# Outputs and gates by feature instead of by token, with the norm's factors sent through DRAM

## The chip, the cores and the metric

The kernel runs on one core of a Trainium2 chip. The metric is device time in microseconds (us) of one execution; lower is better. Beside the runs there is one profiled execution, whose trace gives each instruction's start and length on the engines: PE (TensorE; PEld is its weight load), DVE (VectorE), ACT (ScalarE), POOL (GpSimd), and SP (SyncE), which here issues nearly all DMAs.

## The reference, cut to what matters

x has 16 samples of 128 tokens and 256 features. A small attention layer makes h from x. Then comes the part that the change is in, a gated delta rule with 16 key heads and 32 value heads of 128 features each; two value heads share a key head. Its result is normalised over the 128 features of a head, weighted, gated by silu(z), and projected back to 256 features:

```python
mixed = hidden_states @ W_qkv
z = (hidden_states @ W_z).reshape(b, s, NV, DV)
beta = jax.nn.sigmoid(hidden_states @ W_b)
g = -jnp.exp(A_log) * jax.nn.softplus(hidden_states @ W_a + dt_bias)
mixed = jax.nn.silu(_causal_conv(mixed, conv_w))
...
core = _chunk_gated_delta_rule(q, k, v, g, beta)
core = core * jax.lax.rsqrt(jnp.mean(core * core, axis=-1, keepdims=True) + EPS) * norm_w
core = core * jax.nn.silu(z)
return core.reshape(b, s, VAL_DIM) @ W_out
```

Inside the rule, q and k are divided by their lengths, and each sample's 128 tokens need the inverse of a triangular 128x128 matrix for each head. Two feed-forward layers follow. All is float32.

## The kernel before

The work of the delta rule is cut into 64 units. A unit is one key head (`kh`) and one group of four samples (`g`), which makes eight pairs (`NP`, sample and value head) of 128 tokens. Every unit goes through the same stages, and the main loop (L872) is a software pipeline: in slot n, unit n does its first stage (`keys`, L451), unit n-1 its decays, unit n-7 (`MERGE`) the merging of the inverse and its values, unit n-8 (`OUT`) its outputs (L750), and unit n-10 (`LAST`) its projection (`finish_unit`, L801). Within a slot `plan` gives each step a time on a scale of 24, and the steps are written out in the order of these times. A scheduler then moves single instructions, so that the built program's order on an engine is near the plan but not the same. Each engine runs its own instructions in the built order and waits where an operand or a buffer isn't ready. Buffers turn over in pools: `ps_b` has six buffers of PSUM that almost every product takes one of.

The inverse of the triangular matrices is done for four units at once, on 32x32 blocks, by DVE with some help of POOL (`inverse`, L566). It is spread over two slots in every four: `first` in slot n where n-5 is a multiple of four, `second` in the slot after.

The steps that the change touches, in a unit's order:

- `square` and `norms` (L465, L469): ACT squares keys and queries, PE adds over the features by a product with a matrix of ones 32 columns wide, one for each block of 32 tokens. The sums come out on 32 partitions for each block, all alike; DVE's 32x32 transpose (`turned`, L475) turns them so that a partition holds the sums of its own token. `factors` (L477) makes nn of the query's sum on POOL, 128x4.
- `logarithms` (L498): one block on ACT with the table of exponent and logarithm, for three units at once: the decays of unit n-1, r of unit n-9 (r to the power -1/2 by Ln and Exp), lk and kn of unit n. All silu of the slot stand before or after the block, since they need another table.
- `gate` (L755): z = silu(h W_z), tokens on partitions, two samples to a call; four matmuls with 256 moving columns each. A float32 matmul of the program stands in the profile as two instructions.
- `new_values` (L766), `attend` (L776): PE forms y and then the output of the rule, tokens on partitions, four pairs to a call. ACT squares each pair from PSUM and adds up along the features (`accum_out`, one more instruction each) into r, 128x8. DVE multiplies by z.
- `root` (L790): POOL adds nn to r. `norm` (L795): POOL multiplies z by r, which is one number for each token and pair.
- `turn` (L806): PE transposes z's eight 128x128 tiles, ACT copies them to SBUF as zT, scaled by the norm's weight `nw`, which is one number for each feature. `project` (L813): PE multiplies zT by W_out and adds up over the key heads in PSUM.

On SP the loads of weights (w_qk, w_v, w_gate, wo_head), of decays (aT, 512 KB to all partitions) and the moves of blocks of 32 columns (diag, W, T) stand in one queue, in the built order; an issue that waits holds back those behind it.

Of the kernel before, what the change touches and what calls it, by code (L numbers as in the profile page):

```python
# [56 lines left out]
def tile_adaln_attn_ffn(  # L57
# [80 lines left out]
    sums = dram.tile([NG, NK * NP, S], F32, name="sums")  # L138

# [7 lines left out]
    def attention():  # L147
# [144 lines left out]
        def output(g):  # L292
# [14 lines left out]
            def logs():  # L307
# [12 lines left out]
                V.tensor_tensor(a, ps[:, :, NV:], dtb[:, None, :].to_broadcast([P, GS, NV]), ALU.add)  # L320
                A.activation(sp, sp, AF.Ln, bias=one)
# [129 lines left out]
    def keys(u):  # L451
# [17 lines left out]
        def norms():  # L469

            ps = ps_b.tile([P, 2 * GS, BL], F32, name="ps_n", tag="b")
            for b in BLOCKS:
                T.matmul(ps[b], lhsT=ones, rhs=d["sqa"][:, :, :, b], start=True, stop=True)
            d["tr"] = pc.tile([P, 2 * GS, BL], F32, name="turned", tag="turned")
            V.transpose(out=d["tr"].rearrange("p s t -> p (s t)"), in_=ps.rearrange("p s t -> p (s t)"))  # L475

        def factors():  # L477
            tr = d["tr"][:, :, 0].rearrange("p (s j) -> p j s", j=2)

            nn = d["nn"] = pc.tile([P, GS], F32, name="nn", tag="nn", bufs=10)  # L480
            G.tensor_scalar(nn, tr[:, 1, :], 1e-6, P * P * 1e-6, ALU.add, ALU.mult)  # L481
# [14 lines left out]
        return [lambda: qk(0), lambda: qk(1), lambda: silu(0), lambda: silu(1), square, norms, factors, fade]  # L496

    def logarithms(new, old, done):  # L498
# [17 lines left out]
        if new:  # L516
            block.append(A.activation(lk, un[new]["tr"][:, :, 0].rearrange("p (s j) -> p j s", j=2)[:, 0, :], AF.Ln, bias=small))
            block.append(A.activation(kn, lk, AF.Exp, scale=0.5))
# [231 lines left out]
    def outputs(u):  # L750
# [4 lines left out]
        def gate(n):  # L755
            if n == 0:
                d["z"] = late["p"].tile([P, NP, S], F32, name="z", tag="z", bufs=3)
            ps = ps_b.tile([P, 2, 2 * S], F32, name="ps_z", tag="b")
            for j in range(2):
                t0 = (2 * n + j) * S  # L760
                for c in range(ND):
                    T.matmul(ps[:, j, :], lhsT=hTs[g][:, c, t0 : t0 + S], rhs=w_gate[u][:, c, :],  # L762
                             start=c == 0, stop=c == ND - 1)
            silu_of(d["z"][:, 4 * n : 4 * n + 4, :].rearrange("p q f -> p (q f)"), ps.rearrange("p s f -> p (s f)"))
# [11 lines left out]
        def attend(n):  # L776
            ps = ps_b.tile([P, 4, S], F32, name="ps_ot", tag="b")
            for j in range(4):
                p = 4 * n + j
                T.matmul(ps[:, j, :], lhsT=d["aT"][:, p, :], rhs=d["y"][:, p, :], start=True, stop=True)  # L780
            if n == 0:
                d["r"] = late["p"].tile([P, NP], F32, name="r", tag="r", bufs=2)
            for j in range(4):
                p = 4 * n + j
# [3 lines left out]
            V.tensor_tensor(z, ps, z, ALU.mult)  # L788

        def root():  # L790

            r = d["r"].rearrange("p (s h) -> p s h", h=2)
            G.tensor_tensor(r, r, d["nn"][:, :, None].to_broadcast([P, GS, 2]), ALU.add)

        def norm():  # L795
            G.tensor_tensor(d["z"], d["z"], d["r"][:, :, None].to_broadcast([P, NP, S]), ALU.mult)  # L796

        return [lambda: gate(0), lambda: gate(1), lambda: new_values(0), lambda: new_values(1),
                lambda: attend(0), lambda: attend(1), root], norm

    def finish_unit(u):  # L801
# [4 lines left out]
        def turn(n):  # L806
            ps = ps_b.tile([P, 4, S], F32, name="ps_zt", tag="b")
            for j in range(4):
                T.transpose(ps[:, j, :], d["z"][:, 4 * n + j, :], ident)
            d["zT", n] = late["p"].tile([P, 4, S], F32, name="zT", tag="zT", bufs=2)  # L810
            A.activation(d["zT", n], ps, AF.Copy, scale=nw)  # L811

        def project(n):  # L813
# [3 lines left out]
            for j in range(2):  # L817
                for h in range(2):
                    T.matmul(ps[:, j, :], lhsT=d["zT", n][:, 2 * j + h, :], rhs=w_o[u][:, h, :],  # L819
                             start=kh == j == h == 0, stop=kh == NK - 1 and j == h == 1)  # L820
# [10 lines left out]
        return [lambda: turn(0), lambda: turn(1), lambda: project(0), lambda: project(1)]  # L831
# [40 lines left out]
    for n in range(N + LAST):  # L872
# [298 lines left out]
```

## Time and profile before

| What | us |
| --- | --- |
| runs, median (lowest to highest of 3) | 2407.47 (2407.19 to 2407.93) |
| the profiled execution's own time | 2408.48 |
| its span, first to last instruction | 2406.8 |
| PE busy in the span | 2194.9 (91%) |
| PEld busy | 1432.5 (60%) |
| DVE busy | 1605.2 (67%) |
| ACT busy | 1482.6 (62%) |
| POOL busy | 755.0 (31%) |
| DMA, share of 16 engines (hardware queue) | 22.2% |

Three parts follow one another: the attention stage and the first units' first stages (to about 310 us), the steady pipeline of slots (to about 1980 us), and the feed-forward layers (from about 2020 us). A busy share is a mean over all three. In the lists of instructions a line reads: line of the kernel, engine, operation, output tile <- input tiles, shapes, count | busy us in all, mean ns of one | idle time of the engine just before, and what ended it. In a timeline a line begins with its start and its length, both in us, and ends in brackets with the idle time before it and what released it. Matmuls overlap one another by some 0.15 us, so what a step takes on PE is read from its start to the next step's start.

### The profile page before, as it was taken

The page shows a single profiled execution, that of the slowest core. Times are in us where ns is not written, and L with a number is a line of the kernel's source. Part 1 is how long each engine was busy: PE and PEld are TensorE (multiplying, and loading weights), DVE is VectorE, ACT ScalarE, POOL GpSimd, SP SyncE. Part 2 cuts the span into 40 slices and gives each one's busy share as a digit, 9 for nine tenths or more (in the row PEclk, how much of TensorE's full clock was granted, in tenths as well). Part 3 has the DMA queues.
Part 4 walks back from the last instruction along what each step waited for, and adds up shares of the span by engine and source line. Part 5 has one row for each costly group of instructions (what it writes and reads, how often), then busy time and mean ns, then how long its engine had stood idle before and what let it go on. Part 6 is the DMA issues. An engine that isn't in the chain of part 4 may idle for free. (4 is left out here: it accounts for less than half of the span.)

```text
span 2406.8 us, 41884 instructions
## 1 busy us (share of the span) xinstructions
PE 2194.9 (91%) x16248; PEld 1432.5 (60%) x16248; DVE 1605.2 (67%) x2094; ACT 1482.6 (62%) x3382; POOL 755.0 (31%) x575
## 2 busy tenths in 40 slices
PE   6898588989999998989999998989899898999999
PEld 3443255766666666767666666767666776344445
DVE  4677879687887869697887869696877831311111
ACT  4666576867777686868677776768677774111110
POOL 4555423243323324143323323242323213600000
PEclk9899889999999999999999999999999999999999
DMA  2200031323323332323232232323222324000000
GB/s 57 91 14 23 22 89 51 76 66 81 72 65 80 84 83 61 77 66 83 75 87 71 62 78 61 87 64 80 74 79 68 82 57 145 5 1 20 9 1 18
DMA packets 289908, 148.35 MB, mean 62 GB/s; under 512 B 184240, under 2 KB 278192, under 8 KB 289712
## 3 DMA queue, kind: packets, MB, share of 16 engines
q1 hardware_dynamic: 287792, 141.44, 22.2%
q0 software_dynamic: 1344, 4.20, 0.5%
q8 instruction: 130, 2.13, 0.4%
q14 instruction: 66, 0.54, 0.1%
q10 hardware_dynamic: 576, 0.05, 0.0%
HBM read 119.13 MB, written 5.51 MB: 52 GB/s over the span
## 5 line engine op out<-in xcount | busy, mean ns | idle before, releaser
L446 DVE SCALAR_TENSOR_TENSOR cv<-ps_in,cw,cv 128x500 f32<-128x500 f32 (+2 forms) x768 | 548.1, 737 | 62.8 <-ACT cv L444 51.3
L435 PE MATMUL ps_in<-hT,w_qk 128*128 128x512 f32 x512 | 274.1, 660 | 20.8 <-PE ps_lo L688 7.0
L444 ACT ACTIVATE cv<-ps_in,cw 128x512 f32<-128x512 f32 x256 | 174.7, 682 | 159.1 <-PE ps_in L435 154.1
L762 PE MATMUL ps_z<-w_gate,hT 128*128 128x256 f32 x1024 | 258.5, 387 | 12.3 <-DVE cv L446 12.3
L435 PE MATMUL ps_in<-hT,w_v 128*128 128x512 f32 x512 | 247.7, 607 | 5.0 <-DVE z L788 3.0
L819 PE MATMUL ps_out<-wo_head,zT 128*128 128x256 f32 x1024 | 245.7, 380 | 1.2 <-ACT zT L811 1.2
L819 PEld LDWEIGHTS ps_out<-wo_head,zT 128*128 128x128 f32 x1024 | 192.8, 191 | 53.5 <-issue 28.3
L788 DVE TENSOR_TENSOR z<-ps_ot,z 128x512 f32<-128x512 f32 x128 | 87.5, 684 | 201.9 <-ACT sq L786 201.9
L762 PEld LDWEIGHTS ps_z<-w_gate,hT 128*128 128x128 f32 x1024 | 180.3, 190 | 35.8 <-DVE cv L446 14.5
L796 POOL TENSOR_TENSOR z<-z,r 128x1024 f32<-128x1024 f32 x64 | 148.9, 2327 | 139.6 <-ACT r L515 123.7
L481 POOL TENSOR_SCALAR nn<-turned 128x4 f32<-128x4 f32 x64 | 12.5, 196 | 561.3 <-DVE turned L475 560.8
L786 ACT ACTIVATE sq<-ps_ot 128x128 f32<-128x128 f32 x512 | 142.1, 278 | 58.1 <-PE ps_ot L780 52.1
L597 POOL TENSOR_TENSOR prod<-inv,gm 128x2048 f32<-128x2048 f32 x16 | 89.0, 5564 | 230.7 <-DVE gm L644 230.7
L435 PEld LDWEIGHTS ps_in<-hT,w_v 128*128 128x128 f32 x512 | 96.8, 198 | 106.6 <-issue 96.9
L435 PEld LDWEIGHTS ps_in<-hT,w_qk 128*128 128x128 f32 x512 | 94.7, 206 | 97.6 <-issue 77.8
L549 PE MATMUL ps_kq<-kq 128*128 128x256 f32 x512 | 138.0, 393 | 10.2 <-DVE cv L446 9.7
L780 PE MATMUL ps_ot<-y,aT 128*128 128x128 f32 x1024 | 138.9, 280 | 1.2 <-ACT y L774 1.2
L553 DVE TENSOR_TENSOR bT<-ps_kq,aT 128x512 f32<-128x512 f32 x128 | 87.5, 684 | 77.2 <-PE ps_kq L549 71.5
L780 PEld LDWEIGHTS ps_ot<-y,aT 128*128 128x128 f32 x1024 | 132.7, 196 | 10.0 <-ACT y L774 2.2
L773 PEld LDWEIGHTS ps_y<-v,W 128*128 128x128 f32 x1024 | 119.8, 192 | 23.5 <-issue 20.2
L597 DVE TENSOR_TENSOR prod<-lanes,inv 128x512 f32<-128x512 f32 (+1 forms) x48 | 131.2, 2738 | 0.5
L773 PE MATMUL ps_y<-v,W 128*128 128x128 f32 x1024 | 130.5, 281 | 0.0
(209 smaller groups left out, 4590.3 us busy)
## 6 DMA issues: line engine op xcount, KB each, us to landing
aT<-sums SPq DMA_DIRECT2D x64, 512.0 KB, 4.2
w_qk<-in_w_qkv_dram SPq DMA_DIRECT2D x128, 128.0 KB, 2.3
w_v<-in_w_qkv_dram SPq DMA_DIRECT2D x64, 256.0 KB, 2.9
w_gate<-in_w_z_dram SPq DMA_DIRECT2D x64, 256.0 KB, 2.7
wo_head<-in_w_out_dram SPq DMA_DIRECT2D x64, 256.0 KB, 3.0
diag<-bT SPq DMA_DIRECT2D x256, 32.0 KB, 2.0
W<-Uc SPq DMA_DIRECT2D x256, 32.0 KB, 2.0
T<-Tc SPq DMA_DIRECT2D x128, 32.0 KB, 2.0
```

The source lines that it names most:

```text
L435: T.matmul(ps, lhsT=w[:, c, blk, :], rhs=hTs[g][:, c, :], start=c == 0, stop=c == ND - 1)
L444: A.activation(cv, psv, AF.Copy, scale=cw[:, col, 3:4])
L446: V.scalar_tensor_tensor(out=cv[:, :, sh:], in0=psv[:, :, : S - sh], scalar=cw[:, col, 3 - sh : 4 - sh], in1=cv[:, :, sh:], op0=ALU.mult, ...
L549: T.matmul(ps[:, j, :, :], lhsT=d["kq"][:, s, 0, :], rhs=d["kq"][:, s, :, :], start=True, stop=True)
L553: V.tensor_tensor(d[name][:, 4 * n : 4 * n + 4, :].rearrange("p (s h) t -> p s h t", h=2), ps[:, :, j : j + 1, :].to_broadcast([P, 2, 2, S ...
L597: engine.tensor_tensor(out_tile, lhs[:, :, None, :].to_broadcast([P, r, c, j]), rhs.rearrange("p j c -> p c j")[:, None, :, :].to_broadcas ...
L762: T.matmul(ps[:, j, :], lhsT=hTs[g][:, c, t0 : t0 + S], rhs=w_gate[u][:, c, :], start=c == 0, stop=c == ND - 1)
L773: T.matmul(ps[:, j, :], lhsT=d["W"][:, p, :], rhs=v[:, p, :], start=True, stop=True)
L780: T.matmul(ps[:, j, :], lhsT=d["aT"][:, p, :], rhs=d["y"][:, p, :], start=True, stop=True)
L786: A.activation(sq, ps[:, j, :], AF.Square, accum_out=d["r"][:, p : p + 1])
L796: G.tensor_tensor(d["z"], d["z"], d["r"][:, :, None].to_broadcast([P, NP, S]), ALU.mult)
L819: T.matmul(ps[:, j, :], lhsT=d["zT", n][:, 2 * j + h, :], rhs=w_o[u][:, h, :], start=kh == j == h == 0, stop=kh == NK - 1 and j == h == 1)
```

## The change

Outputs and gates are now computed with features on partitions and tokens along the columns. `gate` and `attend` take one value head to a call with all four samples (512 columns) instead of two samples with both heads. With features on partitions, the weight `nw` can be applied by DVE in the same instruction that multiplies by z, and `project` can take z as it is: the transposes and their copies go. But the sum of squares now runs over partitions: ACT squares 512 columns at a time into `sq` (in the buffer that `square` uses too, tag `sqa`), PE adds up by the product with ones (in `root`, new), and DVE adds nn, which is now kept as 128x4x32 and made by DVE straight from PSUM. r is 128x256 with all partitions of a block of 32 alike. After ACT's Ln and Exp, `share` (new) writes one row of each block to DRAM, 4 KB in four DMAs, and reads them back to all 128 partitions as `rb` (512 KB), and `norm`, now in `finish_unit`, multiplies z by `rb` on POOL. One clamp of `sp` is added in the attention stage, and nearly all planned times are set anew.

```diff
+    scales = dram.tile([NG * NK, 2, GS, len(BLOCKS), BL], F32, name="scales")
...
+                V.tensor_scalar(sp, sp, 3e38, None, ALU.min)
...
-                T.matmul(ps[b], lhsT=ones, rhs=d["sqa"][:, :, :, b], start=True, stop=True)
-            d["tr"] = pc.tile([P, 2 * GS, BL], F32, name="turned", tag="turned")
-            V.transpose(out=d["tr"].rearrange("p s t -> p (s t)"), in_=ps.rearrange("p s t -> p (s t)"))
-
-        def factors():
-            tr = d["tr"][:, :, 0].rearrange("p (s j) -> p j s", j=2)
-
-            nn = d["nn"] = pc.tile([P, GS], F32, name="nn", tag="nn", bufs=10)
-            G.tensor_scalar(nn, tr[:, 1, :], 1e-6, P * P * 1e-6, ALU.add, ALU.mult)
+                T.matmul(ps[b], lhsT=ones, rhs=d["sqa"][:, :, :, b].rearrange("p s j t -> p j s t"), start=True, stop=True)
+            d["tr"] = pc.tile([P, GS, BL], F32, name="turned", tag="turned")
+            ps = ps.rearrange("p (j s) t -> p j (s t)", j=2)
+            V.transpose(out=d["tr"].rearrange("p s t -> p (s t)"), in_=ps[:, 0, :])
+
+            nn = d["nn"] = pc.tile([P, GS, BL], F32, name="nn", tag="nn", bufs=9)
+            V.tensor_scalar(nn.rearrange("p s t -> p (s t)"), ps[:, 1, :], 1e-6, P * P * 1e-6, ALU.add, ALU.mult)
...
-        def gate(n):
-            if n == 0:
-                d["z"] = late["p"].tile([P, NP, S], F32, name="z", tag="z", bufs=3)
-            ps = ps_b.tile([P, 2, 2 * S], F32, name="ps_z", tag="b")
-            for j in range(2):
-                t0 = (2 * n + j) * S
-                for c in range(ND):
-                    T.matmul(ps[:, j, :], lhsT=hTs[g][:, c, t0 : t0 + S], rhs=w_gate[u][:, c, :],
-                             start=c == 0, stop=c == ND - 1)
-            silu_of(d["z"][:, 4 * n : 4 * n + 4, :].rearrange("p q f -> p (q f)"), ps.rearrange("p s f -> p (s f)"))
+        def gate(h):
+            if h == 0:
+                d["z"] = late["p"].tile([P, 2, GT], F32, name="z", tag="z", bufs=3)
+            ps = ps_b.tile([P, GT], F32, name="ps_z", tag="b")
+            for c in range(ND):
+                T.matmul(ps, lhsT=w_gate[u][:, c, h * P : (h + 1) * P], rhs=hTs[g][:, c, :],
+                         start=c == 0, stop=c == ND - 1)
+            silu_of(d["z"][:, h, :], ps)
...
-        def attend(n):
...
-            for j in range(4):
-                p = 4 * n + j
-                sq = late["p"].tile([P, S], F32, name="sq", tag="sq")
-                A.activation(sq, ps[:, j, :], AF.Square, accum_out=d["r"][:, p : p + 1])
-            z = d["z"][:, 4 * n : 4 * n + 4, :]
-            V.tensor_tensor(z, ps, z, ALU.mult)
+        def attend(h):
+            ps = ps_b.tile([P, GT], F32, name="ps_ot", tag="b")
+            for s in range(GS):
+                T.matmul(ps[:, s * S : (s + 1) * S], lhsT=d["y"][:, 2 * s + h, :], rhs=d["aT"][:, 2 * s + h, :],
+                         start=True, stop=True)
+            if h == 0:
+                d["sq"] = pa.tile([P, 2, GS, S], F32, name="sq", tag="sqa")
+            A.activation(d["sq"][:, h].rearrange("p s t -> p (s t)"), ps, AF.Square)
+            z = d["z"][:, h, :]
+            V.scalar_tensor_tensor(out=z, in0=ps, scalar=nw, in1=z, op0=ALU.mult, op1=ALU.mult)
 
         def root():
...
+            ps = ps_b.tile([P, 2, GS, BL], F32, name="ps_r", tag="b")
+            for b in BLOCKS:
+                T.matmul(ps[b], lhsT=ones, rhs=d["sq"][:, :, :, b], start=True, stop=True)
+            r = d["r"] = late["p"].tile([P, 2, GS, BL], F32, name="r", tag="r")
+            V.tensor_tensor(r, ps, d["nn"][:, None, :, :].to_broadcast([P, 2, GS, BL]), ALU.add)
+
+        def share():
+
+            to = scales[index[u]]
+            for i, b in enumerate(BLOCKS):
+                nc.sync.dma_start(out=to[:, :, i, :], in_=d["r"][b.start : b.start + 1])
+            t = d["rb"] = late["p"].tile([P, 2, GT], F32, name="rb", tag="rb")
+            nc.sync.dma_start(out=t.rearrange("p h t -> p (h t)"),
+                              in_=to.rearrange("h s b t -> (h s b t)").partition_broadcast(P))
...
-        def turn(n):
-            ps = ps_b.tile([P, 4, S], F32, name="ps_zt", tag="b")
-            for j in range(4):
-                T.transpose(ps[:, j, :], d["z"][:, 4 * n + j, :], ident)
-            d["zT", n] = late["p"].tile([P, 4, S], F32, name="zT", tag="zT", bufs=2)
-            A.activation(d["zT", n], ps, AF.Copy, scale=nw)
+        def norm():
+            G.tensor_tensor(d["z"], d["z"], d["rb"], ALU.mult)
...
-                    T.matmul(ps[:, j, :], lhsT=d["zT", n][:, 2 * j + h, :], rhs=w_o[u][:, h, :],
+                    T.matmul(ps[:, j, :], lhsT=d["z"][:, h, s * S : (s + 1) * S], rhs=w_o[u][:, h, :],
                              start=kh == j == h == 0, stop=kh == NK - 1 and j == h == 1)
...
-            plan(steps, [2, 2, 7.5, 12] if at(MERGE) else [12])
+            plan(steps, [0, 2, 7.5, 9] if at(MERGE) else [9])
-            plan(keys(at(0)), [1, 5, 5.5, 10.0, 12.0, 14, 15, 18])
+            plan(keys(at(0)), [1, 5, 5.5, 8, 11.5, 14, 18])
-            plan([lambda: logarithms(at(0), at(1), at(OUT + 1))], [15])
+            plan([lambda: logarithms(at(0), at(1), at(OUT + 1))], [14.5])
-            plan(decays(at(1))[:2], [18.0, 21])
+            plan(decays(at(1))[:2], [18.5, 22.5])
-            plan(decays(at(2))[2:], [7])
+            plan(decays(at(2))[2:], [0.5])
-            plan(values(at(MERGE)), [5.5, 8.0, 13, 16.5, 19, 24])
+            plan(values(at(MERGE)), [6.5, 7.5, 12, 15.5, 22, 23])
-            plan(outputs(at(OUT))[0], [13, 20, 16, 17, 19, 22, 23.5])
+            plan(outputs(at(OUT))[0], [11.5, 19, 16, 16, 18.5, 21])
-            plan([outputs(at(OUT + 1))[1]], [17.0])
+            plan(outputs(at(OUT + 1))[1], [0.5, 16])
-            plan(finish_unit(at(LAST)), [7, 7.5, 11.5, 18.5])
+            plan(finish_unit(at(LAST)), [0.5, 7.5, 16.5])
-            plan(second, [4.5, 5.5, 7, 9, 10, 14.5, 17, 23.5])
+            plan(second, [2.5, 6.5, 8, 10.5, 11, 19.5, 20, 24])
```

More of the change, by code (lines that the diff above doesn't have):

```diff
@@ L494, in fade @@
                             fill=-1e30, base=0, channel_multiplier=-1)
-        return [lambda: qk(0), lambda: qk(1), lambda: silu(0), lambda: silu(1), square, norms, factors, fade]
+        return [lambda: qk(0), lambda: qk(1), lambda: silu(0), lambda: silu(1), square, norms, fade]
     def logarithms(new, old, done):
@@ L516, in logarithms @@
         if new:
-            block.append(A.activation(lk, un[new]["tr"][:, :, 0].rearrange("p (s j) -> p j s", j=2)[:, 0, :], AF.Ln, bias=small))
+            block.append(A.activation(lk, un[new]["tr"][:, :, 0], AF.Ln, bias=small))
             block.append(A.activation(kn, lk, AF.Exp, scale=0.5))
@@ L774, in new_values @@
             A.copy(d["y"][:, 4 * n : 4 * n + 4, :], ps)
-        def attend(n):
-            ps = ps_b.tile([P, 4, S], F32, name="ps_ot", tag="b")
-            for j in range(4):
-                p = 4 * n + j
-                T.matmul(ps[:, j, :], lhsT=d["aT"][:, p, :], rhs=d["y"][:, p, :], start=True, stop=True)
-            if n == 0:
-                d["r"] = late["p"].tile([P, NP], F32, name="r", tag="r", bufs=2)
-            for j in range(4):
-                p = 4 * n + j
-                sq = late["p"].tile([P, S], F32, name="sq", tag="sq")
-                A.activation(sq, ps[:, j, :], AF.Square, accum_out=d["r"][:, p : p + 1])
-            z = d["z"][:, 4 * n : 4 * n + 4, :]
-            V.tensor_tensor(z, ps, z, ALU.mult)
@@ L790, in root @@
-        def root():
[L792 to L796, printed above, removed]
+        def attend(h):
[8 more added lines that the diff above has]
+            V.scalar_tensor_tensor(out=z, in0=ps, scalar=nw, in1=z, op0=ALU.mult, op1=ALU.mult)
@@ L798, in outputs @@
         return [lambda: gate(0), lambda: gate(1), lambda: new_values(0), lambda: new_values(1),
-                lambda: attend(0), lambda: attend(1), root], norm
+                lambda: attend(0), lambda: attend(1)], [root, share]
     def finish_unit(u):
@@ L804, in finish_unit @@
         d = un[u]
-        def turn(n):
-            ps = ps_b.tile([P, 4, S], F32, name="ps_zt", tag="b")
-            for j in range(4):
-                T.transpose(ps[:, j, :], d["z"][:, 4 * n + j, :], ident)
-            d["zT", n] = late["p"].tile([P, 4, S], F32, name="zT", tag="zT", bufs=2)
-            A.activation(d["zT", n], ps, AF.Copy, scale=nw)
+        def norm():
+            G.tensor_tensor(d["z"], d["z"], d["rb"], ALU.mult)
         def project(n):
@@ L817, in project @@
             for j in range(2):
+                s = 2 * n + j
                 for h in range(2):
-                    T.matmul(ps[:, j, :], lhsT=d["zT", n][:, 2 * j + h, :], rhs=w_o[u][:, h, :],
+                    T.matmul(ps[:, j, :], lhsT=d["z"][:, h, s * S : (s + 1) * S], rhs=w_o[u][:, h, :],
                              start=kh == j == h == 0, stop=kh == NK - 1 and j == h == 1)
@@ L829, in project @@
                 del un[u]
-        return [lambda: turn(0), lambda: turn(1), lambda: project(0), lambda: project(1)]
+        return [norm, lambda: project(0), lambda: project(1)]
     def ffn_loads():
```

## The prediction

> **What bounds the kernel now.** I read the page's first part, then the stretch table by units, then the timelines of PE, DVE and ACT in the stretch that is longest. Between about 310 and 1980 us the plan feeds one unit per slot. The table has four slots in a row (they repeat as a cycle; columns: stretch, length, then busy us of PE, PEld, DVE, ACT, POOL, granted clock, DMA share, GB/s):
>
> ```profile
> 547.00:571.50 24.50, 24.50 (x225) 17.82 (x224) 13.69 (x20) 19.84 (x49) 5.46 (x6) 1.00 0.31 78
> 571.50:596.10 24.60, 24.60 (x226) 17.84 (x225) 23.44 (x37) 19.95 (x49) 8.48 (x6) 1.00 0.32 86
> 596.10:630.90 34.80, 27.26 (x225) 18.99 (x224) 34.74 (x33) 20.27 (x49) 15.22 (x9) 0.90 0.16 44
> 630.90:656.00 25.10, 24.89 (x227) 17.88 (x228) 14.81 (x22) 19.96 (x49) 6.49 (x8) 1.00 0.40 87
> ```
>
> Three slots are PE's: busy all their 24.5 us. The third row holds the second half of a batch's triangular inverse: there DVE is busy 34.74 of 34.80 us and PE waits. DVE's load starts a slot earlier (23.44 of 24.60), so the burst must be followed as a chain:
>
> ```profile
> 572.37 2.30 DVE L446 SCALAR_TENSOR_TENSOR cv<-ps_in,cw,cv 128x508 f32<-128x508 f32 x3
> ...
> 623.13 0.44 DVE L475 STREAM_TRANSPOSE turned<-ps_n 128x256 f32<-128x256 f32 x1
> ```
> ```profile
> 623.61 0.30 ACT L517 ACTIVATE lk<-turned,small 128x4 f32<-128x4 f32 x1 [3.70 <-DVE turned L475]
> ...
> 625.44 0.63 ACT L533 ACTIVATE cv<-cv 128x512 f32<-128x512 f32 x1
> ```
> ```profile
> 600.02 1.05 PE L688 MATMUL ps_lo<-Tc,bT 32*32 32x32 f32 x30 [3.69 <-DVE z L788]
> ...
> 626.12 0.55 PE L743 MATMUL ps_vt<-ident,cv 128*128 128x128 f32 x3 [1.29 <-ACT cv L533]
> ```
>
> From 572.37 DVE has no gap; at 623.57 it ends `turned`, ACT takes lk, a table load and the silu, and PE is released at 626.12 for the last time. So a cycle of 108.9 us (starts of the long slots at 596.1 and 705.1) is 51.2 us of DVE (572.37 to 623.57), 2.5 us of ACT, and some 55 us of PE: 4.8 left of the long slot, then the slots of 25.1 and 24.5. There are 15 long slots.
>
> **The change part by part: PE.** The light slot at 1201 shows each step's wall time as start to next start:
>
> ```profile
> 1205.36 0.60 PE L809 MATMUL ps_zt<-ident,z 128*128 128x128 f32 x4
> 1205.89 0.21 PE L699 MATMUL ps_up<-Uc,Mi 32*32 32x32 f32 x1
> ...
> 1206.52 0.66 PE L809 MATMUL ps_zt<-ident,z 128*128 128x128 f32 x4
> 1207.02 1.88 PE L435 MATMUL ps_in<-hT,w_v 128*128 128x512 f32 x4
> 1208.73 1.89 PE L819 MATMUL ps_out<-wo_head,zT 128*128 128x256 f32 x8
> ...
> 1213.56 0.64 PE L473 MATMUL ps_n<-sqa,ones 128*32 128x256 f32 x8
> 1214.13 2.05 PE L773 MATMUL ps_y<-v,W 128*128 128x128 f32 x16
> ```
>
> Removed: the eight transposes, 0.53 + 0.50 = 1.03 us a unit. Added: `ps_r`, the same four products with ones over 256 columns as `ps_n`: 0.57. The gates stream the same columns in half as many matmuls: before 1.93 (1211.63 to 1213.56) + 0.45 + 1.30 = 3.68, after two groups of four 512-wide ones as `ps_in`, 1.71 each (1207.02 to 1208.73) = 3.42, or 1.81 each by the w_qk rows = 3.62: -0.26 to -0.06. `attend` and `project` only swap operands. Sum -0.5 to -0.7 us a slot. Against it: `attend(0)` took samples 0 and 1 and so only the first copy of y; now it takes all samples and waits for both. Lining up ACT's slot (silu 0.60, table load 1.28, aT 1.06, r, y 0.57, r, lk, y) behind the gate, which ends about 1.1 us earlier, the second y is ready at 16.4 us of the slot and PE is there at 16.2: 0.2 us lost, 0 to 0.6 by how exact that is. I take -0.5 net in a full light slot, -0.9 in the one after the burst (25.1 us: PE waited there 0.2 for zT), -0.7 in the 4.8 us piece. PE's part of a cycle: -2.1.
>
> **DVE.** A unit gains the add of r (128x256 from PSUM; the rows are 0.28 for 128x128 at L342 and 0.68 for 128x512, L788: 0.41 between), nn on DVE (0.28 by L342), and z as a scalar_tensor_tensor (0.75 by L1065 against 0.68, twice: +0.14); `turned` halves from 0.44 (0.22 if it scales, 0.44 if not). Sum +0.6, bounds +0.5 and +0.9. In the built order the burst from the first cv to `turned` holds one r add (the others fall outside it), one nn, two smaller transposes and two z: 0.41 + 0.28 - 0.44 + 0.14 = +0.4 us, and otherwise the same instructions. The four clamps of sp (about 0.28 each, as L339) lie in the attention stage beside PE.
>
> POOL disturbs the burst: the 512-wide products of L597 took 1.06 us with POOL idle and about 2.0 to 3.1 beside a POOL operation, while cv, bT, z keep their times. The norm multiply (1.9 us of POOL) stood at 591.65 and 619.57, beside L597 both times. Now it runs at the head of a slot, in the burst beside the second pair of 512-wide products, where before aT and its select ran; these move earlier, beside the first pair, which POOL disturbs anyhow. I take -0.4; bounds -2 (both pairs of costs gone) and +2 (a whole norm beside the 128x2048 product, 3.75 us and undisturbed so far). So DVE's part is 0, with -1.6 and +2.4 as ends.
>
> **ACT, hidden.** Out go two zT copies (0.68) and eight squares with accumulator reads (142.1 + 104.0 us over 64 units: 3.85); in come two squares of 128x512 (0.59 as L533's z) and r as 256 columns instead of 8 (+0.2 each): 20 becomes 16.4 of 24 us, under PE. Were it PE's wait it would be a gain, which I don't count beyond the two places above.
>
> **SP, DMA and POOL: the new wait.** `share` issues four writes to DRAM and a read:
>
> ```profile
> aT<-sums SPq DMA_DIRECT2D x64, 512.0 KB, 4.2
> ...
> diag<-bT SPq DMA_DIRECT2D x256, 32.0 KB, 2.0
> ```
> ```profile
> 600.59 2.56 SPq L562 DMA_DIRECT2D diag<-bT  x4
> ```
>
> The writes wait for ACT's r (15.6 us of a slot), issue in 2.56 as four diag do, land 2.0 later; w_gate and aT, ahead of the read on SP, wait for PE until 20.3. The read goes at 20.6, lands at 24.8 as aT does (512 KB both), POOL multiplies for 1.9 (up to 3.6 beside DVE): z is ready at 27 to 28.6. Its reader `project(0)` stands at 6.5 of the next slot, 30.3: 1.7 to 3.4 us to spare; in the long slots more. Queued behind the read on SP are w_out, a part of W, four diag, w_qk and w_v, each wanted 3 us or more later; behind POOL's wait the aT chain and, in the long slot, the inverse's products; behind DVE's r add the cv of the next slot, which PE's `ps_in` releases later anyway. Five issues more bring SP from some 10 to 13 us of 24. At the end nothing covers the trip: last `ps_ot` to `ps_out` took 8.9 us (2010.2 to 2019.15); now squares and silu 3, ps_r and add 1.2, Ln and Exp 1, writes 4.6, read 4.6, norm 2 = 16: +7.
>
> [...]
>
> **The sum.** 14 cycles of -2.1 = -29; the five 19-us slots after the last burst and the first three, -0.5 each = -4; the end +7: -26. From the span of 2406.8: 2380.8. The run's own time is 2408.48 and the runs' median 2407.47, 0.7 over the span, so I write 2381.
>
> **The rivals.** *The burst takes it back* (13%): if the norm lands beside the 128x2048 product, a cycle gets +2.4 on DVE against -2.1 on PE: 14 x 0.3 - 4 + 7 = +7, 2415; for it, DVE is full for 51 us and POOL's order puts the norm right there; against it, the norm needs only 2 us between two such products. Half of that price gives about 2400. *The trip is late* (12%), the slower side: one mechanism, at `project(0)`, from the point where writes, read and norm take over 1.7 to 3.4 us more than reckoned; each us beyond is PE's in some 60 slots. One us: 2381 + 60 = 2441. For it: aT's landings, 4.2 in the middle, and two 2.0 us trips in series; against it: w_gate and aT, not the writes, hold the read. *More than the sum* (11%): PE's wait of 3.69 us vanishes, since in the long slot `ps_ot` and gates no longer hold PSUM beside two `ps_zt`, and L597 runs free: -2 more a cycle, 2381 - 28 = 2353. For it: four causes of PE's waits there; against: DVE is full, so a wait only moves.
>
> [...]
>
> **How the numbers follow.** Forecast 64%: 2381, its own range 2366 to 2398. Range 2358 to 2420: it takes in the first rival and most of the third, and leaves out the late trip. About 0.2% (5 us) can be told from no change. Faster: forecast, third rival and little of the first, 0.74; same 0.07; slower 0.19.
>
> **What would show it.** Light slots of 23.8 to 24.1 us with PE full; no `ps_zt`, `ps_r` about 0.57; the burst from cv to `turned` within 2 us of 51.2; ACT near 16.5 us a slot; PE's wait before `ps_ot` for y under 0.6; the norm ended before `project(0)`. It is wrong if PE waits for POOL's z in light slots, if the long slot exceeds 36 us, or if r's write to DRAM lands after more than 4 us.

## The result, and the profile after

| | before | after |
|---|---|---|
| time, median of 4 runs (range) | 2407.33 us (2403.82 to 2407.93) | 2424.95 us (2421.56 to 2429.74) |
| ratio to before, 95% interval | | 1.0078 (1.0057 to 1.0098) |
| span of the profiled execution | 2406.8 | 2419.8 |
| start to the first long slot (PE's first `ps_lo` there) | 373.2 | 374.0 |
| from there, 56 slots (14 cycles) | 1521.1 | 1522.6 |
| the four slots after them | 84.4 | 90.5 |
| the rest | 428.1 | 432.7 |

The change made the kernel slower by 0.8%; 2381 was predicted, and a range of 2358 to 2420. The profiled execution of after is its fastest run (2421.56), so the stretches show 13.0 us of some 18: +0.8, +1.5, +6.1 and +4.6. Slots are numbered here by the unit that PE merges in them: slot 3 is the first long one, and from slot 57 on no unit does its first stage, so that slots are about 19 us long. The +1.5 flatters the cycles. In the first pair of inverse slots work only moved across the border between the two (21.1 + 39.9 us before, 25.7 + 34.9 after); the 52 slots behind it, 4 to 55, took 1418.6 us and then 1424.1, or 0.4 more a cycle. The 3.8 us that the stretch ahead of that pair became shorter were not followed.

The stretch table of after, four slots of the cycle that the prediction showed for before (columns: stretch, length, busy us of PE, PEld, DVE, ACT and POOL with instruction counts, granted clock, DMA share, GB/s):

```profile
542.20:566.60 24.40, 24.40 (x217) 15.71 (x216) 14.07 (x22) 17.85 (x32) 5.57 (x4) 1.00 0.41 108
566.60:593.20 26.60, 24.58 (x217) 15.63 (x216) 24.77 (x39) 17.85 (x32) 10.12 (x5) 1.00 0.39 106
593.20:626.60 33.40, 26.48 (x217) 15.91 (x217) 33.34 (x33) 18.77 (x33) 13.08 (x6) 1.00 0.24 70
626.60:651.00 24.40, 24.39 (x216) 15.81 (x216) 16.52 (x26) 17.40 (x31) 4.75 (x6) 1.00 0.38 87
```

The light slots (first and last row) are still PE's, at 24.4 instead of 24.5 and 25.1. The two slots of the inverse (the middle rows) take 60.0 instead of 59.4: some 2 us moved from the long slot into the first, where PE now waits for DVE's aT. In every fourth cycle the pair went from some 60.3 to 62.3. So 0.7 us is won in the light slots of a cycle, and the pair takes back 0.6 in an ordinary cycle and 2 in every fourth.

**PE in a light slot.** The timeline of PE in after, the stretch that the prediction showed with the two groups of transposes (start, busy us, engine, line, operation, out<-in, shapes, count):

```profile
1201.10 1.88 PE L437 MATMUL ps_in<-hT,w_v 128*128 128x512 f32 x4
1202.91 0.21 PE L699 MATMUL ps_up<-Uc,Mi 32*32 32x32 f32 x1
...
1203.54 1.98 PE L437 MATMUL ps_in<-hT,w_v 128*128 128x512 f32 x4
1205.36 1.89 PE L821 MATMUL ps_out<-wo_head,z 128*128 128x256 f32 x8
```

Before, a w_v group took 1.71 from start to next start, with transposes beside it; now both take 1.81 and 1.82, the first ahead of products on 32x32 tiles and the second behind them. All stages of the slot that starts at 1198.65, from start to next start, against before: transposes 1.02 to 0, `ps_r` +0.57, the w_v groups 3.44 to 3.63, the w_qk groups 3.63 to 3.73, `ps_vt` +0.04, gates 3.67 to 3.63: -0.16 in sum.

**DVE and POOL in the burst.** The burst is DVE's work from the first cv of the first inverse slot to `turned`. In the cycle looked at it went from 51.2 to 52.2 us:

```profile
1115.04 2.30 DVE L448 SCALAR_TENSOR_TENSOR cv<-ps_in,cw,cv 128x508 f32<-128x508 f32 x3 [1.90 <-ACT cv L446]
...
1166.97 0.30 DVE L478 STREAM_TRANSPOSE turned<-ps_n 128x128 f32<-128x128 f32 x1
```

The groups of before and after by form, products of the inverse on DVE (busy us and mean ns of one, then idle):

```profile
L597 DVE TENSOR_TENSOR Tc<-inv,gm 128x1024 f32<-128x1024 f32 x16 | 84.6, 5286 | 0.0
L597 DVE TENSOR_TENSOR prod<-inv,gm 128x512 f32<-128x512 f32 x32 | 54.4, 1730 | 0.1
```
```profile
L597 DVE TENSOR_TENSOR Tc<-inv,gm 128x1024 f32<-128x1024 f32 x16 | 105.6, 6603 | 0.0
L597 DVE TENSOR_TENSOR prod<-inv,gm 128x512 f32<-128x512 f32 x32 | 40.7, 1294 | 0.0
```

The second pair of 512-wide products got cheaper by 0.87 us, as the prediction had hoped; the first pair (prod<-lanes,inv) got dearer by 0.27, and the 1024-wide one by 1.3. The timelines of one long slot of after show why, POOL's and then DVE's:

```profile
1157.99 5.54 POOL L597 TENSOR_TENSOR prod<-inv,gm 128x2048 f32<-128x2048 f32 x1 [14.37 <-DVE gm L644]
```
```profile
1156.70 1.21 DVE L644 TENSOR_REDUCE gm<-Tc 128x128 f32<-128x1024 f32 x1
...
1158.48 6.79 DVE L597 TENSOR_TENSOR Tc<-inv,gm 128x1024 f32<-128x1024 f32 x1
```

And the same of before:

```profile
1158.69 5.57 POOL L597 TENSOR_TENSOR prod<-inv,gm 128x2048 f32<-128x2048 f32 x1 [13.97 <-DVE gm L644]
```
```profile
1156.34 2.27 DVE L644 TENSOR_REDUCE gm<-prod 128x128 f32<-128x2048 f32 x1
...
1161.06 4.98 DVE L597 TENSOR_TENSOR Tc<-inv,gm 128x1024 f32<-128x1024 f32 x1
```

In before DVE's product starts 2.37 us behind POOL's, in after 0.49 us, because the new order puts the sum gm<-Tc last, and POOL's product waits for both sums. Both end about 1.75 us after POOL's product: 1166.04 against 1164.26, and 1165.27 against 1163.53. DVE's product ends as if it had stood still until POOL was through: alone it takes 1.93 us (f1 below).

Behind `turned` the chain is as it was, ACT's lk and then its silu with a table load of 1.28 us between them, in after's timeline of ACT:

```profile
1167.31 0.30 ACT L517 ACTIVATE lk<-turned,small 128x4 f32<-128x4 f32 x1 [5.17 <-DVE turned L478]
...
1169.14 0.63 ACT L533 ACTIVATE cv<-cv 128x512 f32<-128x512 f32 x1
```

From the end of `turned` to the end of the long slot 6.93 us pass, 7.37 before.

**The 19-us slots.** From slot 57 on, PE's timeline has a wait that before did not have, in slots 57, 58 (0.64 us, not shown), 60 and 62 (idle before an instruction in brackets, with what ended it):

```profile
1861.73 1.99 PE L821 MATMUL ps_out<-wo_head,z 128*128 128x256 f32 x8 [1.08 <-POOL z L812]
...
1933.04 3.72 PE L821 MATMUL ps_out<-wo_head,z 128*128 128x256 f32 x16 [2.03 <-POOL z L812]
...
1973.57 1.99 PE L821 MATMUL ps_out<-wo_head,z 128*128 128x256 f32 x8 [1.29 <-POOL z L812]
```

The trip behind the last of these, in SP's timeline and POOL's:

```profile
1961.44 2.68 SPq L798 DMA_DIRECT2D scales<-r  x4
...
1966.06 0.41 SPq L800 DMA_DIRECT2D rb<-scales  x1
```
```profile
1971.16 2.35 POOL L812 TENSOR_TENSOR z<-z,rb 128x1024 f32<-128x1024 f32 x1 [17.18 <-DMA rb<-scales]
```

From the first write's issue to the norm 9.7 us pass, and 2.35 more until z is ready. A slot of 24 us hides that; one of 19 does not. The four waits are 5.0 us in sum. Of the 6.1 us that slots 59 to 62 grew by, 3.3 are two of them; most of the rest lies in slots 59 and 60, around the end of the last burst, where the kernel without the trip (e2 below) is no faster (52.7 us against 51.2).

### The profile page after: what moved, and what is told of

Read it like the earlier page. It is cut to its first block, busy times and chain, and to the rows that moved or that the text cites. A ratio compares the mean times of both kernels' runs of the same rounds, so it can differ in the third digit from the quotient of the medians.

```text
span 2419.8 us, 40623 instructions
## 1 busy us (share of the span) xinstructions
PE 2202.9 (91%) x15736; PEld 1298.1 (54%) x15736; DVE 1638.3 (68%) x2226; ACT 1356.2 (56%) x2359; POOL 731.6 (30%) x447
## 5 line engine op out<-in xcount | busy, mean ns | idle before, releaser
L812 POOL TENSOR_TENSOR z<-z,rb 128x1024 f32<-128x1024 f32 x64 | 153.3, 2395 | 393.8 <-DMA rb<-scales 313.1
L821 PE MATMUL ps_out<-wo_head,z 128*128 128x256 f32 x1024 | 248.8, 387 | 15.1 <-POOL z L812 15.0
L760 PE MATMUL ps_z<-hT,w_gate 128*128 128x512 f32 x512 | 254.2, 618 | 1.1 <-DVE cv L448 1.1
L821 PEld LDWEIGHTS ps_out<-wo_head,z 128*128 128x128 f32 x1024 | 193.2, 194 | 69.4 <-issue 27.7
L777 PEld LDWEIGHTS ps_ot<-aT,y 128*128 128x128 f32 x1024 | 136.4, 195 | 81.3 <-DVE cv L448 35.8
L777 PE MATMUL ps_ot<-aT,y 128*128 128x128 f32 x1024 | 144.9, 283 | 33.6 <-DVE cv L448 27.5
L553 DVE TENSOR_TENSOR bT<-ps_kq,aT 128x512 f32<-128x512 f32 x128 | 87.1, 680 | 127.1 <-PE ps_kq L549 84.4
L783 DVE SCALAR_TENSOR_TENSOR z<-ps_ot,nw,z 128x512 f32<-128x512 f32 x128 | 94.8, 743 | 108.2 <-ACT sq L781 107.9
L487 POOL TENSOR_TENSOR o<-off,lk 128x16 f32<-128x16 f32 x64 | 23.1, 360 | 461.0 <-ACT lk L517 461.0
L533 ACT ACTIVATE kq<-cv 128x512 f32<-128x512 f32 x128 | 80.1, 626 | 86.7 <-DVE cv L448 86.5
L746 ACT ACTIVATE v<-ps_vt,kn 128x256 f32<-128x256 f32 x256 | 105.2, 475 | 41.3 <-PE ps_vt L743 41.2
```

The lines of the kernel that those rows point to most:

```text
L746: A.activation(d["v"][:, s, :, :], ps[:, j, :, :], AF.Copy, scale=d["kn"][:, s : s + 1])
L760: T.matmul(ps, lhsT=w_gate[u][:, c, h * P : (h + 1) * P], rhs=hTs[g][:, c, :], start=c == 0, stop=c == ND - 1)
L777: T.matmul(ps[:, s * S : (s + 1) * S], lhsT=d["y"][:, 2 * s + h, :], rhs=d["aT"][:, 2 * s + h, :], start=True, stop=True)
L783: V.scalar_tensor_tensor(out=z, in0=ps, scalar=nw, in1=z, op0=ALU.mult, op1=ALU.mult)
L812: G.tensor_tensor(d["z"], d["z"], d["rb"], ALU.mult)
L821: T.matmul(ps[:, j, :], lhsT=d["z"][:, h, s * S : (s + 1) * S], rhs=w_o[u][:, h, :], start=kh == j == h == 0, stop=kh == NK - 1 and j == h ...
```

## The experiments

Fourteen kernels, each timed against the kernel before on the same chip (its median 2407.5 to 2409.2). "Pair" is the two slots of the inverse; burst and products are those of one cycle, a product's length from its start to the next start, unless a mean is named.

**The transposes: e3_no_turn.** The kernel before, edited:

```diff
-            ps = ps_b.tile([P, 4, S], F32, name="ps_zt", tag="b")
-            for j in range(4):
-                T.transpose(ps[:, j, :], d["z"][:, 4 * n + j, :], ident)
-            d["zT", n] = late["p"].tile(...)
-            A.activation(d["zT", n], ps, AF.Copy, scale=nw)
+            d["zT", n] = d["z"][:, 4 * n : 4 * n + 4, :]
```

> The kernel before without the transposes of z and the copies that take them out of PSUM; the projection takes z as it lies. Left out: the turning of z, and the weight that its copy multiplies in. Theory A (the transposes also separated a 512-wide group from products on 32 rows, and that cover is lost with them, so they are worth less than their 1.03 us): a light slot goes from 24.54 to about 23.9 us, -0.5 to -0.7. Theory B (the prediction's way to cost them: the wall time of the transposes goes whole): 23.5 us, -1.0. The long slots, which DVE and ACT set, keep about 34.9 us in both; 42 light slots give -20 to -30 by A and -43 by B.

Measured: 2386.76 us, ratio 0.9902 (0.9886 to 0.9919). The light slot is 23.72, -0.82: between the two theories. PE's timeline has the same three rows as after:

```profile
1193.84 1.88 PE L435 MATMUL ps_in<-hT,w_v 128*128 128x512 f32 x4
1195.65 0.21 PE L699 MATMUL ps_up<-Uc,Mi 32*32 32x32 f32 x1
...
1196.28 1.98 PE L435 MATMUL ps_in<-hT,w_v 128*128 128x512 f32 x4
1198.10 1.89 PE L815 MATMUL ps_out<-wo_head,z 128*128 128x256 f32 x8
```

The two w_v groups take 3.63 here and 3.44 before, with nothing changed but the transposes: 1.02 - 0.20 is the 0.82. Theory A's mechanism holds, with a loss of 0.20 where it was given 0.3 to 0.5. The long slots did not keep 34.9: they are 36.6 to 39.2, the burst 53.3 instead of 51.2. In it the second pair of 512-wide products is 1.9 us shorter, but the first pair is 1.9 longer, Tc<-inv,gm 0.7 and the small products ahead of them 1.5: POOL's norm, Tc and aT lie beside others than before. More than half of what PE won in 14 cycles went there.

**The trip: e2_no_trip and e4_one_write.** The kernel after, edited in `share`:

```diff
 e2_no_trip
-            to = scales[index[u]]
...
+            d["rb"] = late["rb"]
 e4_one_write
-            for i, b in enumerate(BLOCKS):
-                nc.sync.dma_start(out=to[:, :, i, :], in_=d["r"][b.start : b.start + 1])
+            nc.sync.dma_start(out=to.rearrange("h s b t -> b (h s) t"),
+                              in_=d["r"].rearrange("p h s t -> p (h s) t")[0 : P : BL])
```

> The kernel after without the four writes to DRAM and the read back: the norm multiplies by a constant tile of ones. Left out: the factor of the outputs (and its transport); everything else, the norm's multiply on POOL too, is as it was. Theory A (the trip costs only where slots are 19 us long, and at the end, where nothing covers it): the slots from 57 on lose PE's waits for the norm, 1.1 + 0.6 + 2.0 + 1.3 = 5 us, and the last chain about 9 us; the slots 3 to 59 keep 1522.6 us within 4; time about 2411 us (2408 to 2415). Theory B (the rival of the prediction: the trip is late everywhere, or its issues hold up SP's queue): the slots 3 to 59 also shorten, by 0.3 us or more each, and the time falls below 2400 us.

> The kernel after with the four writes of the factors to DRAM made by one DMA of the same pieces. Theory A (the trip has no slack in the 19-us slots and at the end, and three issues of about 0.65 us are in its way): PE's waits for the norm from slot 57 on shrink by about 2 us each, the end by 2 us: 5 to 8 us less in all, about 2418 us; the slots 3 to 59 unchanged. Theory B (the issue isn't what makes the trip long; the landing of 128-byte pieces is): one DMA with all the pieces lands later by what the issue gains, and the time stays within 2 us.

Measured: e2 2405.86 us, ratio 0.9984 (0.9975 to 0.9994); e4 2410.76 us, 1.0002 (0.9993 to 1.0012). Theory A of e2 is right in place: from slot 3 to the start of slot 59 it takes 1523.8 (1522.6 with the trip), the light slot that PE fills is 24.38 in both, and the slots from 57 on have no wait for the norm. The edit isn't a clean one, since the norm now starts at other times: the slot after the burst fell from 24.5 to between 22.8 and 24.0, and the pair rose from a mean of 60.7 to 62.0. The profiled executions differ by 11.6 us in span, and what lies behind slot 63 went from 432.7 to 421.0. By the ratios the gain is larger than theory A's 14, some 22 us. The profiles, one execution each, do not show the rest; the one of after was its fastest run (2421.56), the one of e2 its slowest (2410.21). Without any trip the change gains only 0.2%, so the trip is not what ate most of the forecast's 29 us. In e4 the way from write to norm is 7.1 us instead of 9.7:

```profile
1957.23 0.56 SPq L797 DMA_DIRECT2D scales<-r  x1
...
1960.17 0.41 SPq L800 DMA_DIRECT2D rb<-scales  x1
```
```profile
1964.36 2.35 POOL L812 TENSOR_TENSOR z<-z,rb 128x1024 f32<-128x1024 f32 x1 [16.24 <-DMA rb<-scales]
```

The write issues in 0.56 and not 2.68, the read follows 2.94 us behind its start and not 4.62, and the norm starts 4.2 and not 5.1 behind the read. Theory A, and by the ratios more of it than the 5 to 8 us expected. The edit also moved the sum gm<-Tc forward: the burst fell to 50.55.

**The burst: e1_sum_early, f1_all_dve, f4_before_all_dve, f2_pool_after, f5_before_pool_after.**

```diff
 e1 (on after)
-            plan(second, [2.5, 6.5, 8, 10.5, 11, 19.5, 20, 24])
+            plan(second, [2.5, 6.5, 2.5, 10.5, 11, 19.5, 20, 24])
 f1 (on e4), f4 (on before)
-                times(t, *args, G if part else V)
+                times(t, *args, V)
 f2 (on e4), f5 (on before); the same for Tc, in merge8
+                if part and second:
+                    V.memset(full[:, 0:1], 0.0)
                 times(t, *args, G if part else V)
```

> The kernel after, with one due time changed: in the second half of the inverse, the first sum of the first pair of products is issued earlier, so that POOL's product starts well ahead of DVE's next one, as it did before the change, and the two overlap less. Theory A (the lost time of the burst is DVE and POOL working side by side: L597 rose from 4.90 to 6.71 us at the stretch looked at): that product falls back to about 5 us, the burst from the first cv to turned goes from 52.2 to 50.4 us, and 15 long slots give 20 to 25 us: about 2400 us. Theory B (what DVE loses beside POOL on one product it gets back on the next, so that the order is indifferent): the parts shift between the two products, the burst stays within 0.5 us of 52.2 and the time within 5 us of 2425.

Measured: 2420.61 us, 1.0044 (1.0029 to 1.0058). POOL's product now starts 1.72 us ahead of DVE's:

```profile
1153.73 5.57 POOL L597 TENSOR_TENSOR prod<-inv,gm 128x2048 f32<-128x2048 f32 x1 [12.63 <-DVE gm L644]
```
```profile
1155.45 5.63 DVE L597 TENSOR_TENSOR Tc<-inv,gm 128x1024 f32<-128x1024 f32 x1
```

Tc<-inv,gm falls to 5.54 where theory A had about 5, the burst to 51.1: the 1.1 us of that product and no more. The direction is A's, its size and the 20 to 25 us are not, for a cycle gains far less than the burst. In means over 13 cycles:

| | burst | `turned` to the slot's end | pair |
|---|---|---|---|
| before | 51.3 | 7.5 | 59.6 |
| after | 52.7 | 7.1 | 60.7 |
| e1 | 51.8 | 7.9 | 60.5 |
| e4 | 51.4 | 8.8 | 61.0 |
| g3 (below) | 50.6 | 7.0 | 58.5 |

With the burst back near its old length PE is late with its own work behind `turned`, and the pair stays long. So the longer burst alone doesn't account for the pair. What keeps PE late is not shown. One thing goes with it: the time in a pair in which PE's clock was not granted (length times one minus the granted clock, which at any moment is 1.00 or 0.50 in the traces of before and after; mean over 13 pairs) is 3.6 us before, 3.1 after and 3.4 in e1, but 5.0 in e4 and 2.3 in g3.

> The kernel after with one write for the factors (as e4_one_write), and the two big products of the inverse that POOL took (Tc of 1024 and prod of 2048 elements a lane) given back to DVE. Theory A (a product of two SBUF operands on POOL and one on DVE go one after the other whichever engine has them, so POOL's share frees DVE of nothing): the pair of 512-wide products falls from 4.65 to 2.1 us, Tc<-inv,gm from 5.56 to 1.9, and DVE takes on 1.9 and 3.75: burst 50.55 - 2.55 - 3.66 + 5.65 = 50.0 us; time within 8 us of 2411. Theory B (POOL relieves DVE of what it takes): burst 50.55 + 5.65 = 56.2, 15 long slots of +5 or so: about 2485 us.

> The kernel before with the two big products that POOL took given to DVE. Theory A (one after the other whichever engine has them): the pair of 512-wide products 4.06 to 2.1 us, Tc<-inv,gm 4.90 to 1.9, the other pair 3.88 to between 2.1 and 3.9, and 5.65 more of DVE's own: burst 51.2 - 1.0 to 51.2 + 0.7; time 2395 to 2420. Theory B (POOL relieves DVE): burst about 56, time 2475 or more.

Measured: f1 2414.62 us, 1.0026 (1.0016 to 1.0037); f4 2411.15 us, 1.0008 (0.9999 to 1.0018). Theory A: DVE does 5.65 us or more by itself in addition, and the burst is 51.2 and 52.7 where B had 56. (f4's is above A's 51.9: its first 512-wide pair rose to 5.05 us beside POOL's norm and aT instead of falling to 2.1.) In f1's DVE timeline the product that took DVE 5.56 us beside POOL in e4, and the one that POOL had, are:

```profile
1160.14 1.93 DVE L597 TENSOR_TENSOR Tc<-inv,gm 128x1024 f32<-128x1024 f32 x1
...
1162.62 3.65 DVE L597 TENSOR_TENSOR prod<-inv,gm 128x2048 f32<-128x2048 f32 x1
```

DVE does both in 1.93 + 3.65 = 5.58 us, which is what its own one took beside POOL. POOL's help is worth 0.7 (f1 against e4) and 1.5 us of a burst (f4 against before).

> The kernel after with one write for the factors, and POOL's two products made to wait (by a write of one element into their output tiles) until DVE's own products of two SBUF operands are through, so that they lie beside DVE's work on PSUM and its sums. Theory A (the lost time of the burst is these products side by side): the pair of 512-wide products 2.1 us instead of 4.65, Tc<-inv,gm 1.9 instead of 5.56: burst 44.5 to 46 us against 50.55. The cycle shortens by less, since PE then sets more of it (its busy time is about 101 us of a cycle of 109): 3 to 5 us a cycle, 2340 to 2370 us. Theory B (the products are slow for another reason, or what waits for POOL's product is late by as much): burst above 49, time above 2400.

> The kernel before with POOL's two products made to wait for DVE's, as in f2_pool_after. It shows whether the change is worth anything once the burst no longer takes its gain. Theory A: burst 51.2 - 1.95 - 3.0 = 46.3, a cycle 3 to 5 us shorter, 2345 to 2375 us, and f2_pool_after is faster than this by the light slots' 0.2 to 0.6 us each, some 5 to 20 us, less what the trip costs at the end. Theory B (the change costs something of its own in every cycle): f2_pool_after is slower than this.

Measured: f2 2432.76 us, 1.0097 (1.0080 to 1.0114); f5 2435.91 us, 1.0108 (1.0086 to 1.0131): both slower, though f2's burst ends at `turned` after 48.9 us. Tc<-inv,gm is 1.92 as A said, but POOL needs 5.59 for 2048 elements even undisturbed, and the sum behind it now waits. From DVE's timeline of f2:

```profile
1146.02 6.88 DVE L597 TENSOR_TENSOR prod<-inv,gm 128x512 f32<-128x512 f32 x2
...
1170.85 1.92 DVE L597 TENSOR_TENSOR Tc<-inv,gm 128x1024 f32<-128x1024 f32 x1
...
1179.14 2.29 DVE L651 TENSOR_REDUCE inv<-prod 128x128 f32<-128x2048 f32 x1 [2.34 <-POOL prod L597]
```

The conflict only moved: POOL's Tc and norm (2.86 and 3.20 us, from 1145.96 on) now lie beside the second pair, 2.1 us alone, which lasts 6.88. Theory B, by its second reason: what waits for POOL's product is late. f2 and f5 are alike, so no gain of the change shows there either.

**The due times: h1_old_times and h2_new_times.** The seven lines of due times that both kernels have, put back in after (with those of the outputs), and put into before:

```diff
 h1 (on after), for example
-                plan(values(at(MERGE)), [6.5, 7.5, 12, 15.5, 22, 23])
+                plan(values(at(MERGE)), [5.5, 8.0, 13, 16.5, 19, 24])
```

> The kernel after with the due times of before for every step that both have (merging, keys, logarithms, decays, values, outputs, second half of the inverse); root, share and finish keep those of the change. Theory A (the operations lost the gain: the burst's new ones and POOL's product beside DVE's): the pair of inverse slots stays at 60 to 62 us, the time within 10 us of 2425. Theory B (the new due times lost it): the pair goes to 59.4 or below, light slots stay at 24.4: a cycle of 108.2 or less, 2405 to 2415 us, the trip at the end still paid.

> The kernel before with the due times of the change for the steps that both have, its outputs and its finish as before. Theory A (operations): the pair stays at 59.4 and the time within 8 us of 2408. Theory B (due times): the pair grows to 60 or more, 2420 us or more.

Measured: h1 2455.30 us, 1.0202 (1.0185 to 1.0219); h2 2415.28 us, 1.0029 (1.0016 to 1.0041). With the old times the changed kernel is slower still (light slots 24.9, where PE waits 0.25 for ACT's square ahead of `ps_r`; pairs of 60 to 63.5). For h1 that is theory A's pair, and a time beyond both theories. h2 lies between them: pairs of 59.7 to 62.6, and 7.8 us. So the new times suit the changed kernel, which is 2% slower than before without them. But they are not free: in the kernel before, with none of the new operations, they make the pair longer by 0.9 us on average (60.5 against 59.6), nearly as much as the whole change does (60.7). How much of the pair's growth is due to the times and how much to the operations these two runs don't separate.

**What would beat both: g1_first_dve, g2_act, g3_both, g4_before_both.** All on e4, g4 on before; the one-element copy stands at the end of merge8(True) and holds Tc back:

```diff
 g1, g3, g4
-                times(t, *args, G if part else V)
+                times(t, *args, G if part and second else V)
...
+                V.tensor_copy(bt["T"][:, 0, 0:1], st_["X"][:, 8 * BL : 8 * BL + 1])
 g2, g3 (g4 the first of the two)
-            V.tensor_copy(W[c, :, e], ps[1][c])
+            A.copy(W[c, :, e], ps[1][c])
-            V.tensor_scalar(nn..., ps[:, 1, :], 1e-6, P * P * 1e-6, ALU.add, ALU.mult)
+            A.activation(nn..., ps[:, 1, :], AF.Copy, scale=P * P * 1e-6, bias=P * P * 1e-12)
```

> The kernel after with one write for the factors (e4_one_write), and the first of POOL's two products of the inverse given to DVE, held back behind the second pair of 512-wide products (by a copy of one element into its output tile). bT and aT of the first inverse slot are then not behind a pair of products that POOL slows. Theory A (PE's wait of 2.2 us for DVE's aT in the first inverse slot, and the half clock after it, are work that PE has left over when the burst ends): that wait vanishes, the slot goes from 26.6-28.3 to about 24.5 us, the two inverse slots together from about 60.2 to 58, 15 times: about 2385 us. Theory B (only the length of the burst counts): the pair 4.65 to 2.1 and 1.9 more for DVE, burst 50.55 to about 50.0, about 2403 us.

> The kernel after with one write for the factors, and two small operations taken from DVE to ACT: the copy of W out of PSUM (0.42 us, twice in the burst) and nn (0.2 of DVE's time). Theory A (DVE sets the burst, each us there is one of the cycle): burst 50.55 to 49.5, 15 times 1.0: about 2396 us. Theory B (PE's leftover work sets the cycle once the burst is under some 51 us): the burst falls by the same, the time by less than 4 us.

> g1_first_dve and g2_act together. By theory A of both: burst about 49 us, 2370 to 2385 us; by theory B of both: 2395 to 2403. It is the candidate that should beat the kernel before (about 2409 on such a chip).

> The kernel before with the same two edits as g3_both, without nn (POOL has it there). The pair of 512-wide products 4.06 to 2.1 us, 2.0 more for the product that POOL gives back, the copies of W -0.84: burst 51.2 to 50.4, about 2397 us. If the change of the case is worth its light slots (0.2 to 0.6 us each), g3_both is faster than this by 5 to 20 us; if the change takes in DVE's part what it gives in PE's, the two are within 5 us.

Measured: g1 2410.56 us, 1.0013 (1.0001 to 1.0025); g2 2424.64, 1.0070 (1.0050 to 1.0090); g3 2392.73, 0.9945 (0.9928 to 0.9961); g4 2441.16, 1.0143 (1.0126 to 1.0160). In g1 PE's wait of 2.2 us did vanish and the first slot is 24.38, but the long one grew to 36.8: neither theory; the wait had only moved. In g2 two operations left DVE's burst, and in the cycle looked at it is 51.2, more than e4's 50.55, because the second 512-wide pair (2.11 to 3.37) and Tc<-inv,gm (5.56 to 6.10) came to lie differently beside POOL. In g4 Tc<-inv,gm is 6.77 and the burst 52.2 where 50.4 was expected; g3 is 48 us faster than g4, beyond what either reading allowed, so the two don't price the change. Only g3 lands where both edits help: burst 49.9, and the fastest kernel of the study that computes the whole reference. Its stretches:

```profile
545.40:569.80 24.40, 24.40 (x217) 15.71 (x216) 13.47 (x20) 18.39 (x34) 5.73 (x5) 1.00 0.39 101
569.80:594.20 24.40, 24.40 (x217) 15.72 (x216) 22.79 (x40) 18.62 (x34) 7.26 (x5) 1.00 0.36 101
594.20:627.50 33.30, 27.97 (x219) 17.54 (x220) 33.30 (x31) 18.93 (x34) 11.91 (x6) 0.90 0.23 69
627.50:651.80 24.30, 24.30 (x217) 15.66 (x216) 15.71 (x24) 18.62 (x34) 5.94 (x6) 1.00 0.44 110
```

106.4 us against 108.8: the first slot of the inverse has no wait, and the long one did not grow in return.

## Why the prediction was wrong

The sum was -26: -29 for 14 cycles, -4 for the first and the 19-us slots, +7 for the end. The spans show +13: +1.5, +6.9 and +4.6. Cut at the start of the first pair of inverse slots, so that no pair is split, the cycles are some +4 instead of -29. That is 2.4 us a cycle, of which PE's part has 1.0 and DVE's part 1.4.

- **"I take -0.4; bounds -2 and +2" for POOL's disturbance** is the step that failed most: it put DVE's part of a cycle at 0, and the burst grew by 1.0 in the cycle looked at and by 1.4 on average. The new operations on DVE were right (+0.4 put; 0.38 in the cycle looked at: nn 0.20, r 0.33, z 0.12, `turned` -0.27). The disturbance was +0.7 there, a burst of 52.2, and more in every fourth cycle, with a burst of 54.4. The prediction looked for it beside the norm, and took two products side by side as two that share; the built order had moved another thing, the sum that starts POOL's product. What counts is when POOL's product ends: DVE's ends 1.73 to 1.79 us later, whether it started 2.37 (before), 1.71 (e4), 0.49 (after) or 0.44 us (g3) behind POOL's. Alone it takes 1.93 us (f1), so in these runs it is as if it began when POOL's was through. f1 agrees, where DVE does both in 5.58 us, and f4, whose burst without POOL's two products is 52.7 us and not about 56. The prediction did not weigh that. That the burst grew for this reason is shown by e1 and f1; that the time would come back with the burst is not, since in e1 and e4 the pair stayed long.
- **"Sum -0.5 to -0.7 us a slot" for PE** failed too: it came out as -0.16. `ps_r` (0.57) was as priced, and the gates (-0.04) came just short of the low end of what they were given (-0.06). The transposes were costed by their own wall time; e3 shows that 0.20 of their 1.02 comes back in the w_v groups, which they had kept apart from the 32x32 products, and in after another 0.10 comes back in w_qk, beside the new `ps_r`. The slot after the burst (-0.9 put, 25.0 to 24.48 measured) and the piece behind `turned` (-0.7 put, 7.37 to 6.93 measured) were nearer. PE's part of a cycle is about -1.1 and not -2.1.
- **"1.7 to 3.4 us to spare" for the trip** was a little high where it was worked out: in the light slot at 1223 the norm ends at 1228.65 and `project(0)` starts at 1229.74, 1.1 us later, without a wait. It was worked out for slots of 24 us alone. The slots from 57 on are 19 us long, the same trip is late by 0.6 to 2.0 us there, and the prediction gave them a gain. The rival "The trip is late" had the mechanism and the wrong extent: four slots, not sixty. Up to the read the trip was as priced: 2.56 us for the issue of the writes and 2.0 to their landing were put, and the read is issued 4.62 us after the first write.
- **The end, +7**, was near for the chain itself. Its last wait, in before and in after:

```profile
2019.15 3.72 PE L819 MATMUL ps_out<-wo_head,zT 128*128 128x256 f32 x16 [0.34 <-ACT zT L811]
```
```profile
2037.26 5.30 PE L821 MATMUL ps_out<-wo_head,z 128*128 128x256 f32 x16 [5.57 <-POOL z L812]
```

From the last `ps_ot` to the end of the last `ps_out` it took 13.1 us before and 22.8 after. The next stage's first product, `ps_low`, starts 9.1 us later after the start of slot 63, and 4.7 of that is won back in the first part of that stage, which takes 69.6 us to its second `ps_low` instead of 74.4. So +4.6 is left, in part by luck.
- Right: no `ps_zt`, no wait for y in light slots, PE full there, ACT down (to 17.9, not 16.5), and DVE's burst as what ends last in the pair of after, though e1 shows PE's own work close behind it. The rival "The burst takes it back" was nearest, at 2415 with the right place; its mechanism, the norm beside the 128x2048 product, does not occur (that product stays at 3.78).

What stays open: why the pair stays long when the burst is short again (e1, e4), and what the new due times have to do with it (h2). By their ratios e2 and e4 gain some 10 us more on after than the profiled executions show, of which some 6 to 8 are due to which execution was profiled. Why every fourth pair is 2 us longer was not followed.

## What to carry to other kernels

Where one engine is full over a long stretch, an order that changes there can weigh more than the operations added or removed: look in the built order for products with two SBUF operands on DVE beside a product on POOL that starts first, and price them by POOL's end plus their own time (here 1.73 to 1.79 us behind POOL's end, and 1.93 alone). Then ask what stands close behind that stretch: here a shorter burst gave little back while PE was late. Price an operation that is taken out together with what stood on either side of it. A trip that one slot hides must be held against the shortest slot in which it runs, and a chain of small DMAs against its issue time first (here 2.68 of the 9.7 us from the first write to the norm).

## What the runs showed of the hardware that was not expected

- POOL's product of 128x2048 takes 5.5 to 5.6 us and DVE's 3.65, and DVE's 128x1024 one 1.93: both together cost DVE 5.58, about what the smaller one costs it beside POOL's (4.90 in before, 5.56 in e4, 6.71 in after).
- DVE's operations with an operand in PSUM (cv, bT, z) and its sums keep their times beside POOL's products: cv has a median of 0.74 to 0.75 us alone and 0.73 to 0.75 beside them, bT 0.69 and 0.68 to 0.69, z 0.75 and 0.73 (in after), a sum over 128x1024 1.20 and 1.20 to 1.21 (in before).
- A 512-wide group of four matmuls takes 1.71 us between groups on 128x128 tiles, and 1.81 to 1.92 where products of 32 or 64 rows, or of 32 columns, stand ahead of it or behind it.
- Four writes of 1 KB from four partitions issue in 2.68 us, one DMA with the same pieces in 0.56.
